# The depthwise conv of a state-space layer as diagonal products on TensorE, with the step's slots laid out anew

## The chip, the cores and the metric

The kernel runs on one core of one Trainium2 chip. A core has five engines that run at the same time and meet through semaphores: TensorE (PE in the profile, with its weight loads listed apart as PEld), VectorE (DVE), ScalarE (ACT), GpSimd (POOL) and SyncE (SP), whose queue issues nearly all transfers here. The metric is the device time of one execution in microseconds, as a median of runs. The kernel before takes 9295.23 us (three runs, 9294.63 to 9299.92).

## The reference, cut to what matters

The network has four layers, each `x = x + layer(groupnorm(x))`, on an input of 8 samples, 384 channels and 32x32 positions: a state-space layer (layer 0), a deformable conv (layer 1), a state-space layer with an MLP behind it (layer 2), and a shift layer (layer 3). The change concerns layer 0 alone. Cut to its core, with L = 1024 tokens, 768 inner channels and 16 states, it is:

```python
xin, z = split(xseq @ in_proj_w.T)                 # 768 channels each
xc = causal_depthwise_conv(xin, conv_w, taps=3) + conv_b
u = silu(xc)
dt, Bm, Cm = split(u @ x_proj_w.T)                 # 24, 16, 16
dt = softplus(dt @ dt_proj_w.T + dt_proj_b)
h[t] = exp(dt[t] * A) * h[t-1] + dt[t] * u[t] * Bm[t]   # per channel and state
y[t] = sum_n h[t, n] * Cm[t, n] + u[t] * D
out = (y * silu(z)) @ out_proj_w.T
```

## The kernel before, in words

**Steps, groups, units.** `ssm_layer` serves both state-space layers. It goes through 16 steps, one for each half (512 tokens) of each of the 8 samples; the first half of a sample is a step with `h` 0, the second one with `h` 1, which carries states and a two-token halo over from the first. A step has six groups `j`, each of 128 inner channels, and a group has eight units `m`. A unit is 32 channels times four states on the 128 partitions, for two state pairs in a 1024-long row. So a step has 48 units, and layer 0 has 768.

**One unit.** ScalarE makes the decays (`decays`, L494: two exponentials of 128x512 into a PSUM tile `da`, of which there are two, taken in turn). GpSimd makes the inputs (`inputs`, L502, a 128x1024 product into `db`, three buffers) and in a step with `h` 1 adds the carry (`add_carry`, L487). VectorE does the recurrence over both (`scan`, L514). Then the states are multiplied by C (`with_c`): by GpSimd (L525) when `m` is in the group's set in `GP_C`, else by VectorE (L527). For GpSimd's units the scan writes to an SBUF tile `hs` (seven buffers); for VectorE's it writes in place in `da`, and the product goes to `hs`. TensorE sums the states of four units into `y` (`read_out`, L537; eight products of 32 columns). The decays of unit i+2 and the inputs of unit i+3 are issued in unit i.

**What is done beside the units.** `plan` gives every other piece of work a slot, 0 to 47, one slot a unit, and an engine queue. All four compute engines take their instructions in exactly that order (`manual_schedule`); in a slot ScalarE's items stand ahead of the decays, VectorE's items behind the scan and the product, TensorE's items ahead of a read-out. Read-outs stand at the end of the slot of unit 5 and of unit 0 of the next group. The items of one step `s` belong to the steps before (`prev`) and after (`nxt`) as well:

- softplus of group j+2 (L408 to L451): `dt_proj` on TensorE in unit 2, four activations in unit 3, `soft_rest` on VectorE in 4, the logarithm in 5; in layer 0 TensorE sums its three parts with an identity matrix (`soft_add`), ScalarE copies the sum out (`soft_take`) and VectorE multiplies it by u (`soft_du`). `spread` then sends both to DRAM and reads them back in the units' layout.
- the gate of group j (`z_proj`, three products; `gate`, silu with a table load, L550; `exp_ln` loads the table of the exponential again, L377), and `close` (L557), which multiplies `y` by it, in unit 2 of the next group.
- for the next step: load and group norm of x, `inner` (L348, three products of 128x128 by 128x512 for each of six channel blocks d), the conv, `silu`, `x_proj`, `x_store` and `load_bc`.
- for the step before: `residual` (load of x), `out_proj` (six products for each of three blocks o) and `out_take` (L589).

**The conv** before is `conv_last` on ScalarE (L352: tap 2 and the bias from PSUM; in a step with `h` 1 three one-column corrections with the halo, L360; in one with `h` 0 the halo is saved, L354) and `conv` on VectorE (L368: two `scalar_tensor_tensor` over 511 and 510 columns, with taps 1 and 0). The same two functions do the first step, ahead of the units, and all of layer 2.

**PSUM.** `da` has two tiles of two banks, `y` one bank, and the pool behind `psum()` three banks, shared by all other products; a new one waits until an old one has been read.

Of the kernel before, what the change touches and what calls it, by code (L numbers as in the profile page):

```python
# [8 lines left out]
F32 = mybir.dt.float32  # L9
AF = mybir.ActivationFunctionType  # L10
ALU = mybir.AluOpType
# [4 lines left out]
P = 128  # L16
# [6 lines left out]
ND = DI // P  # L23
# [3 lines left out]
TS = L // 2  # L27
# [4 lines left out]
IP = P // NI  # L32
NSUB = P // IP
NQP = NS // NI // 2
GP_C = {0: ((0, 2, 4, 6), (0, 2, 5)), 2: ((0, 2, 5), (0, 2, 5))}
PE_SUM = (0,)
ENGINES = {mybir.EngineType.Activation, mybir.EngineType.PE, mybir.EngineType.DVE, mybir.EngineType.Pool}
FF = 4 * C
# [40 lines left out]
V_CW, V_CB, V_DB, V_D, V_A = 0, 18, 24, 30, 36  # L79
# [17 lines left out]
class Net:  # L97
# [107 lines left out]
    def ssm_layer(self, li, src, dst, shift=None):  # L205
        tc, nc, ins = self.tc, self.nc, self.ins
# [4 lines left out]
        with ExitStack() as ctx:  # L211
# [18 lines left out]
            if mlp:  # L230
                w1_d = ins["w1"].rearrange("(k p) o -> p k o", p=P)
                w2_d = ins["w2"].rearrange("(k p) o -> p k o", p=P)
                mean_w = wp.tile([P, P], F32, name="mean_w")
                nc.vector.memset(mean_w, 1.0 / C)
            else:
                win = wp.tile([P, G, 2 * DI], F32, name="win")
                nc.sync.dma_start(out=win, in_=win_d)
                wout = wp.tile([P, ND, C], F32, name="wout")
                nc.sync.dma_start(out=wout, in_=wout_d)
                diag_d = wp.tile([P, ND, P], F32, name="diag_d")  # L240
                for j in range(ND):
                    nc.gpsimd.tensor_scalar(
                        diag_d[:, j, :], self.ident, vec[:, V_D + j : V_D + j + 1], None, ALU.mult
                    )
            nc.sync.dma_start(out=wx, in_=ins[f"wx{li}"].rearrange("(k p) o -> p k o", p=P))
            nc.sync.dma_start(out=wdt, in_=ins[f"wdt{li}"])

# [8 lines left out]
            def v(i):  # L256
                return vec[:, i : i + 1]
# [82 lines left out]
            def inner(s, d):  # L340
                if d == 0:
                    s["u"] = p2.tile([P, ND, TS], F32, name="u", tag="u")
                    if s["h"] == 0:
                        s["sib"]["halo"] = p2.tile([P, ND, 2], F32, name="halo")
                xn, w = s["xn"], s["win", d]
                s["in", d] = ps = self.psum("ps_in")
                for k in range(G):
                    nc.tensor.matmul(ps, w[:, k, :], xn[:, k, :], start=(k == 0), stop=(k == G - 1))  # L348

            def conv_last(s, d):  # L350
                ps, ud = s["in", d], s["u"][:, d, :]
# [152 lines left out]
            def hs_tile(s, m):  # L504
                t = s["hs", m] = p2.tile([P, 2, TS], F32, name="hs", tag="hs", bufs=7)
                return t

            def scan(s, j, m):
                if j == 0 and m == 0 and s["h"] == 0:
                    s["sib"]["st"] = p2.tile([P, ND, NS], F32, name="st")  # L510
                da, db = s["da", m], s["db", m]
                h = hs_tile(s, m) if m in gp_c[j % 2] else da
                h1, da1, db1 = (t.rearrange("p i l -> p (i l)") for t in (h, da, db))
                nc.vector.tensor_tensor_scan(h1, da1, db1, 0.0, ALU.mult, ALU.add)  # L514
                s["h", m] = h
# [5 lines left out]

            def with_c(s, j, m):
                c = s["bc"][m // NSUB][:, 1]
                if m in gp_c[j % 2]:
                    nc.gpsimd.tensor_tensor(s["hs", m], s["hs", m], c, ALU.mult)  # L525
                else:
                    nc.vector.tensor_tensor(hs_tile(s, m), s["da", m], c, ALU.mult)  # L527
# [118 lines left out]

            TG, TS2 = ((8, 8, 24, 24, 31, 47), (24, 31)) if mlp else ((7, 15, 23, 31, 39, 47), (23, 31))
            TZ = (6, 7, 22, 23, 30, 45) if mlp else tuple(t - 1 for t in TG)  # L650
            TI = (16, 17, 18, 24, 25, 26) if mlp else (15, 16, 17, 24, 25, 26)
            NU = NS // 2
            T = ND * NU

            def plan(prev, s, nxt):
                act, dve, pool, pe = queues = [[[] for _ in range(T + NU)] for _ in range(4)]

                def put(q, t, fn, *args):
                    if not args or args[0]:
                        q[t].append((fn, *args))  # L660

                for j in range(ND):
                    t = NU * j
                    put(dve, t + 2, close, *((s, j - 1) if j else (prev, ND - 1)))
                    tz = TZ[j]
                    put(pe, tz - 2, fetch_in, s, ND + j)
                    put(pe, tz, z_proj, s, j)
                    put(act, TG[j], gate, s, j)

                    n, k = (s, j + 2) if j + 2 < ND else (nxt, j + 2 - ND)  # L670
                    put(pe, t + 2, dt_proj, n, k)
                    put(act, t + 3, soft_exp, n, k)
                    put(dve, t + 4, soft_rest, n, k)
                    put(act, t + 5, soft_ln, n, k)
                    if pe_sum:
                        put(pe, t + 5, soft_add, n, k)
                        put(act, t + 6, soft_take, n, k)
                        put(dve, t + 7, soft_du, n, k)
                    else:
                        put(pool, t + 6, soft_sum, n, k)  # L680
                    put(pool, t + 7, spread, n, k)
# [25 lines left out]
                for d, t in enumerate(TI):  # L707
                    put(pe, t - 2, fetch_in, nxt, d)
                    put(pe, t, inner, nxt, d)
                    put(act, t + 1, conv_last, nxt, d)  # L710
                    put(dve, t + 2, conv, nxt, d)
                put(pe, 32 if mlp else 30, x_proj, nxt, 0, ND // 2)
                put(pe, 33 if mlp else 32, x_proj, nxt, ND // 2, ND)
                put(act, 34 if mlp else 33, x_store, nxt)
                for p, t in enumerate((36, 45)):
                    put(pool, t, load_bc, nxt, p)
                put(act, 7 if mlp else 9, residual, prev)
                for o, (t, e) in enumerate(((0, 2), (1, 3), (4, 5)) if mlp else ((8, 9), (10, 11), (12, 13))):
                    if mlp and o < 2:
                        put(pe, (T - 9, T - 6)[o], fetch, nxt and s, "out", o)  # L720
                    else:
                        put(pe, 0, fetch, prev, "out", o)
                    put(pe, t, out_proj, prev, o, 0, ND // 2)
                    put(pe, e, out_proj, prev, o, ND // 2, ND)
                    put(act if mlp else dve, e + (1 if mlp else 2), out_take, prev, o)
# [21 lines left out]
            with tc.manual_schedule(engines=ENGINES):  # L747
# [37 lines left out]
                for i, (s, j, m) in enumerate(units):  # L785
                    c, t = divmod(i, T)
                    if t == 0:
                        queues = plan(
                            steps[c - 1] if c else None, s, steps[c + 1] if c + 1 < len(steps) else None
                        )  # L790
                        for k, q in enumerate(over or ()):
                            for i0, items in enumerate(q):
                                queues[k][i0][:0] = items
                        act, dve, pool, pe = queues
                        over = [q[T:] for q in queues]
                    mine = m in gp_c[j % 2]
                    run(act[t])
                    scan(s, j, m)
                    if not mine:
                        with_c(s, j, m)  # L800
                    keep_last(s, j, m)
                    ahead = units[i + 2] if i + 2 < len(units) else (None, None, None)
                    if ahead[2] == 0:
                        first_token(*ahead[:2])
                    if ahead[0]:
                        decays(*ahead)
                    run(dve[t])
                    if i + 3 < len(units):
                        inputs(*units[i + 3])
                        if ahead[2] == 0:  # L810
                            carry(*ahead[:2])
                            add_carry(*ahead)
                        if units[i + 3][2] > 0:
                            add_carry(*units[i + 3])
                    if mine:
                        with_c(s, j, m)
                    run(pool[t])
                    run(pe[t])
                    for r in late.pop(i, ()):
                        read_out(*r)  # L820
                    if m % NSUB == NSUB - 1:
                        late.setdefault(i + (1 if m == NU - 1 else 2), []).append((s, j, m // NSUB))
# [1113 lines left out]
```

## Time and profile before

The profiled execution took 9297.33 us, of which its instructions span 9295.5 us; 1.8 us lie around them. Layer 0's first scan starts at 75.5 us and its last ends at 2879.5 us.

| stretch (us from the span's start) | length | DVE busy | POOL busy | PE busy | ACT busy | PE clock |
|---|---|---|---|---|---|---|
| whole span | 9295.5 | 83% | 61% | 81% | 70% | 0.88 |
| one step with h 1 (953.29 to 1132.76) | 179.5 | 164.7 | 167.4 | 131.2 | 123.3 | 0.81 |
| one step with h 0 (1132.76 to 1304.90) | 172.1 | 160.2 | 162.2 | 126.6 | 128.3 | 0.81 |

A busy share is a union of instruction spans. TensorE's matmuls are pipelined, and each fp32 product of 128x512 stands in the trace as two records. Start-to-start distances, read off the timeline, are shorter than the durations of the group list, since an instruction's end overlaps the next one's start.

### The profile page before, as it was taken

The numbers are of one execution on the slowest core, as the hardware profiler recorded it, in microseconds if no ns is written. First come the engines' busy times: TensorE is split into PE (matmuls) and PEld (weight loads), VectorE is DVE, ScalarE is ACT, GpSimd is POOL, SyncE is SP. The second block draws the span as 40 slices with busy tenths as digits, with TensorE's granted clock in tenths as the row PEclk, the third lists the DMA queues.
The fourth block names the chain that finished last, engine by engine and source line by source line (L and its number), as shares of the span: only waits on it lengthen the run. The fifth ranks groups of instructions, "written<-read, shape, count | busy, mean of one in ns | idle before, by whom it ended". The sixth has DMA issues, their size and how long they took to land. (4 is left out here: it accounts for less than half of the span.)

```text
span 9295.5 us, 93074 instructions
## 1 busy us (share of the span) xinstructions
PE 7557.6 (81%) x29452; PEld 3856.6 (41%) x29452; DVE 7733.3 (83%) x8617; ACT 6500.3 (70%) x10467; POOL 5645.4 (61%) x3393
## 2 busy tenths in 40 slices
PE   6777677677676999999999997588888888888876
PEld 2222222222223777767777766133333333333333
DVE  6999999999995878878878877788988889898972
ACT  5677677677673878878877876677777677776750
POOL 6999999999994000000000000898989989899964
PEclk7788788788787999999999998798999889999988
DMA  4544544544543333333333333566656666666656
GB/s 123 124 115 113 123 116 114 123 119 114 123 114 81 82 80 85 92 83 85 90 84 86 91 80 85 118 154 151 150 139 155 151 161 147 148 148 145 161 145 112
DMA packets 785233, 1094.47 MB, mean 118 GB/s; under 512 B 274963, under 2 KB 427955, under 8 KB 752985
## 3 DMA queue, kind: packets, MB, share of 16 engines
q1 hardware_dynamic: 722628, 1077.98, 47.6%
q10 hardware_dynamic: 62100, 10.44, 0.7%
q8 instruction: 235, 3.85, 0.2%
q14 instruction: 270, 2.20, 0.1%
HBM read 917.84 MB, written 170.33 MB: 117 GB/s over the span
## 5 line engine op out<-in xcount | busy, mean ns | idle before, releaser
L502 POOL TENSOR_TENSOR db<-dub,bc 128x1024 f32<-128x1024 f32 x1536 | 3603.2, 2355 | 405.9 <-DVE hs L514 224.6
L494 ACT ACTIVATE da<-dtb,vec 128x512 f32<-128x512 f32 x3072 | 2119.5, 691 | 672.9 <-DVE hs L527 416.9
L514 DVE TENSOR_TENSOR_SCAN da<-da,db 128x1024 f32<-128x1024 f32 x912 | 2086.3, 2288 | 258.9 <-ACT da L494 116.4
L435 POOL TENSOR_TENSOR dt<-dt,sp_e 128x512 f32<-128x512 f32 x96 | 122.3, 1274 | 2885.4 <-DMA bc<-bcd 2881.1
L1598 PE MATMUL wacc<-fsm,fxk 128*128 128x221 f32 (+34 forms) x10624 | 1657.2, 315 | 98.1 <-DVE fsm L1568 95.1
L1598 PEld LDWEIGHTS wacc<-fsm,fxk 128*128 128x128 f32 x10624 | 1570.0, 195 | 236.1 <-DVE fsm L1568 159.2
L514 DVE TENSOR_TENSOR_SCAN hs<-da,db 128x1024 f32<-128x1024 f32 x624 | 1423.9, 2282 | 166.4 <-POOL db L487 76.7
L525 POOL TENSOR_TENSOR hs<-hs,bc 128x1024 f32<-128x1024 f32 x624 | 1470.8, 2357 | 15.2 <-ACT st L520 14.9
L1568 DVE TENSOR_TENSOR fsm<-fhy,fhx 128x170 f32<-128x170 f32 (+42 forms) x3216 | 1170.2, 428 | 342.3 <-PE wacc L1598 315.3
L527 DVE TENSOR_TENSOR hs<-da,bc 128x1024 f32<-128x1024 f32 x912 | 1116.9, 1225 | 111.8 <-PE y L537 58.5
L537 PE MATMUL y<-hs,cols 128*32 128x512 f32 x6144 | 826.1, 618 | 160.5 <-POOL hs L525 154.6
L1528 ACT ACTIVATE fhy<-fpyx,cell 128x416 f32<-128x416 f32 (+9 forms) x1280 | 645.5, 576 | 385.0 <-DVE fsm L1568 385.0
L1551 DVE TENSOR_TENSOR fxk<-fxt,fwk 128x1024 f32<-128x1024 f32 (+1 forms) x688 | 787.1, 1179 | 10.2 <-ACT fxt L1330 10.2
L614 PE MATMUL ps_m<-hid,wm 128*128 128x512 f32 x1152 | 550.2, 633 | 61.7 <-ACT hid L609 27.7
L595 PE MATMUL ps_h<-t,wm 128*128 128x512 f32 x1152 | 529.7, 604 | 43.2 <-DVE sp_e L427 25.4
L1533 ACT ACTIVATE fhy<-fhy,cols 128x1344 f32<-128x1344 f32 (+10 forms) x368 | 530.8, 1442 | 12.0
L537 PEld LDWEIGHTS y<-hs,cols 128*32 128x32 f32 x6144 | 171.3, 112 | 798.3 <-issue 497.7
L348 PE MATMUL ps_in<-xn,winr 128*128 128x512 f32 x576 | 328.9, 718 | 174.5 <-ACT xn L337 125.4
L444 PE MATMUL ps_sp<-dt,ident 128*128 128x512 f32 x192 | 168.4, 974 | 290.8 <-ACT dt L414 285.7
L614 PEld LDWEIGHTS ps_m<-hid,wm 128*128 128x128 f32 x1152 | 226.9, 203 | 394.3 <-issue 282.7
L1239 PE MATMUL ps_off<-fxn,fow 128*98 128x465 f32 (+10 forms) x896 | 386.6, 579 | 0.0
L444 PE MATMUL ps_sp<-sp_e,ident 128*128 128x512 f32 x192 | 174.9, 1009 | 259.5 <-DVE sp_e L425 259.5
(212 smaller groups left out, 10436.4 us busy)
## 6 DMA issues: line engine op xcount, KB each, us to landing
dtb<-dtd SPq DMA_DIRECT2D x768, 256.0 KB
dub<-dtd SPq DMA_DIRECT2D x768, 256.0 KB
fpyx<-fposd SPq DMA_DIRECT2D x640, 256.0 KB
wm<-in_w SPq DMA_DIRECT2D x96, 768.0 KB
bc<-bcd SPq DMA_DIRECT2D x256, 256.0 KB
x<-x SPq DMA_DIRECT2D x71, 768.0 KB
dtd<-dt SPq DMA_DIRECT2D x192, 256.0 KB
dtd<-sp_e SPq DMA_DIRECT2D x192, 256.0 KB
```

Of the source, the lines that this page charges most:

```text
L494: nc.scalar.activation(da[:, i, :], s["dtb", j][:, k, :], AF.Exp, scale=na[:, j, n + i : n + i + 1])
L502: nc.gpsimd.tensor_tensor(db, du, s["bc"][p][:, 0], ALU.mult)
L514: nc.vector.tensor_tensor_scan(h1, da1, db1, 0.0, ALU.mult, ALU.add)
L525: nc.gpsimd.tensor_tensor(s["hs", m], s["hs", m], c, ALU.mult)
L527: nc.vector.tensor_tensor(hs_tile(s, m), s["da", m], c, ALU.mult)
L537: nc.tensor.matmul(s["y"][k * IP : (k + 1) * IP, :], sel, s["hs", p * NSUB + k][:, i, :], start=mlp and p == 0 and i == 0, stop=p == NQP - ...
L614: nc.tensor.matmul(ps, s["w2", q][:, f, o * P : (o + 1) * P], s["hid", q][:, f, :], start=(f == 0), stop=(f == 3))
L1528: nc.scalar.activation(hy[:, at : at + (yb - ya) * W], pyx[:, 0, ya * W : yb * W], AF.Abs, bias=bias)
L1533: nc.scalar.activation(hy[:, :at], hy[:, :at], AF.Relu, bias=self.col(Q_ONE), scale=-1.0)
L1551: nc.vector.tensor_tensor(t[:, :n], x, wk[:, j : j + 1, :].to_broadcast([P, n, P]), ALU.mult)
L1568: nc.vector.tensor_tensor(self.sub(sm, at, [(r * w, n), (w, r), (1, w)]), self.sub(hy, hy_at[by] + xa, [(r * W, n), (W, r), (1, w)]), self ...
L1598: nc.tensor.matmul(a[:, ya - 4 * o : yb - 4 * o, xa:xb], k, self.sub(sm, sm_at[by], [(w, yb - ya), (1, w)]), start=False, stop=False,)
```

## The change

In layer 0, for all steps that are planned (not for the first one):

1. **Conv.** ScalarE copies the projection's PSUM tile to u (`conv_in`) and, where `h` is 0, the halo. TensorE multiplies u by three diagonal matrices of the taps, with shifted columns, into a new PSUM tile (`conv_pe`: three products of 128x128 by 512, 511 and 510 columns, and in a step with `h` 1 two more of one and two columns for the halo). ScalarE writes the sum with the bias back to u (`conv_out`). VectorE's `conv` and the one-column corrections go. GpSimd builds the 18 diagonals once at the start.
2. **GP_C.** Groups 0, 2 and 4 gave GpSimd four of their eight products with C, groups 1, 3 and 5 three. Now all six give it three, units 0, 2 and 5; VectorE has the other five. Layer 2 had these sets already and keeps them.
3. **Slots.** Sums of softplus move from unit 5 to 6 of a group and their copy from 6 to 7; gates move from unit 7 to unit 0 of the next group, and their projections from 6 to 7 (the last group's stay in units 5 and 7); the output projection moves from slots 8 to 13 to slots 3 to 9, and `residual` from 9 to 4; the inner projections and the conv are spread over slots 11 to 28, at most one `conv_pe` in a slot; x_proj and x_store come one or two slots later.

```diff
-GP_C = {0: ((0, 2, 4, 6), (0, 2, 5)), 2: ((0, 2, 5), (0, 2, 5))}
+GP_C = {0: ((0, 2, 5),) * 6, 2: ((0, 2, 5),) * 6}
...
+                diag_w = wp.tile([P, 3 * ND, P], F32, name="diag_w")
+                for k in range(3 * ND):
+                    nc.gpsimd.tensor_scalar(
+                        diag_w[:, k, :], self.ident, vec[:, V_CW + k : V_CW + k + 1], None, ALU.mult
+                    )
...
+            def conv_in(s, d):
+                ps, ud = s["in", d], s["u"][:, d, :]
+                nc.scalar.copy(ud, ps)
+                if s["h"] == 0:
+                    nc.scalar.copy(s["sib"]["halo"][:, d, :], ps[:, TS - 2 : TS])
+
+            def conv_pe(s, d):
+                ud = s["u"][:, d, :]
+                s["cv", d] = ps = self.psum("ps_cv")
+                edge = s["h"] == 1
+                nc.tensor.matmul(ps, diag_w[:, 3 * d + 2, :], ud, start=True, stop=False)
+                nc.tensor.matmul(ps[:, 1:], diag_w[:, 3 * d + 1, :], ud[:, : TS - 1], start=False, stop=False)
+                if edge:
+                    halo = s["halo"][:, d, :]
+                    nc.tensor.matmul(ps[:, 0:1], diag_w[:, 3 * d + 1, :], halo[:, 1:2], start=False, stop=False)
+                    nc.tensor.matmul(ps[:, 0:2], diag_w[:, 3 * d, :], halo, start=False, stop=False)
+                nc.tensor.matmul(ps[:, 2:], diag_w[:, 3 * d, :], ud[:, : TS - 2], start=False, stop=True)
+
+            def conv_out(s, d):
+                nc.scalar.activation(s["u"][:, d, :], s["cv", d], AF.Identity, bias=v(V_CB + d))
...
-                h = hs_tile(s, m) if m in gp_c[j % 2] else da
+                h = hs_tile(s, m) if m in gp_c[j] else da
...
-            TG, TS2 = ((8, 8, 24, 24, 31, 47), (24, 31)) if mlp else ((7, 15, 23, 31, 39, 47), (23, 31))
-            TZ = (6, 7, 22, 23, 30, 45) if mlp else tuple(t - 1 for t in TG)
-            TI = (16, 17, 18, 24, 25, 26) if mlp else (15, 16, 17, 24, 25, 26)
+            TG, TS2 = ((8, 8, 24, 24, 31, 47), (24, 31)) if mlp else ((8, 16, 24, 32, 40, 47), (24, 32))
+            TZ = (6, 7, 22, 23, 30, 45) if mlp else (7, 15, 23, 31, 39, 45)
+            TI = (16, 17, 18, 24, 25, 26) if mlp else (11, 12, 17, 18, 20, 24)
+            TCV, TCO = (13, 16, 19, 21, 25, 27), (15, 17, 20, 22, 26, 28)
...
-                        put(pe, t + 5, soft_add, n, k)
-                        put(act, t + 6, soft_take, n, k)
+                        put(pe, t + 6, soft_add, n, k)
+                        put(act, t + 7, soft_take, n, k)
                         put(dve, t + 7, soft_du, n, k)
...
-                    put(act, t + 1, conv_last, nxt, d)
-                    put(dve, t + 2, conv, nxt, d)
-                put(pe, 32 if mlp else 30, x_proj, nxt, 0, ND // 2)
-                put(pe, 33 if mlp else 32, x_proj, nxt, ND // 2, ND)
-                put(act, 34 if mlp else 33, x_store, nxt)
+                    if mlp:
+                        put(act, t + 1, conv_last, nxt, d)
+                        put(dve, t + 2, conv, nxt, d)
+                    else:
+                        put(act, t + 1, conv_in, nxt, d)
+                        put(pe, TCV[d], conv_pe, nxt, d)
+                        put(act, TCO[d], conv_out, nxt, d)
+                put(pe, 32, x_proj, nxt, 0, ND // 2)
+                put(pe, 33, x_proj, nxt, ND // 2, ND)
+                put(act, 34, x_store, nxt)
...
-                put(act, 7 if mlp else 9, residual, prev)
-                for o, (t, e) in enumerate(((0, 2), (1, 3), (4, 5)) if mlp else ((8, 9), (10, 11), (12, 13))):
+                put(act, 7 if mlp else 4, residual, prev)
+                for o, (t, e) in enumerate(((0, 2), (1, 3), (4, 5)) if mlp else ((3, 4), (5, 5), (8, 9))):
```

More of the change, by code (lines that the diff above doesn't have):

```diff
@@ L523, in with_c @@
                 c = s["bc"][m // NSUB][:, 1]
-                if m in gp_c[j % 2]:
+                if m in gp_c[j]:
                     nc.gpsimd.tensor_tensor(s["hs", m], s["hs", m], c, ALU.mult)
@@ L795, in ssm_layer @@
                         over = [q[T:] for q in queues]
-                    mine = m in gp_c[j % 2]
+                    mine = m in gp_c[j]
                     run(act[t])
```

## The prediction

> **What bounds layer 0 now.** First the page: busy time, and the slices of 232 us.
>
> ```profile
> PE 7557.6 (81%) x29452; PEld 3856.6 (41%) x29452; DVE 7733.3 (83%) x8617; ACT 6500.3 (70%) x10467; POOL 5645.4 (61%) x3393
> ...
> DVE  6999999999995878878878877788988889898972
> ...
> POOL 6999999999994000000000000898989989899964
> ```
>
> In slices 2 to 12, layer 0, VectorE and GpSimd are both at nines, while TensorE is at 6 or 7. The chain that ended last is 1% long and lies in layer 3, so it says nothing here. Next the stretches: two whole steps (the first with `h` 1, the second with `h` 0), then groups 1 and 3 of the second one. Columns: length, busy us of PE, PEld, DVE, ACT and POOL, granted clock, DMA share, GB/s.
>
> ```profile
> 953.29:1132.76 179.47, 131.17 (x415) 47.39 (x418) 164.66 (x120) 123.30 (x203) 167.35 (x122) 0.81 0.49 118
> 1132.76:1304.90 172.14, 126.58 (x374) 41.46 (x370) 160.17 (x109) 128.31 (x236) 162.15 (x73) 0.81 0.49 118
> ...
> 1157.83:1186.84 29.01, 27.88 (x85) 10.34 (x84) 27.40 (x19) 20.81 (x37) 29.01 (x13) 1.00 0.47 118
> 1217.21:1249.78 32.57, 25.19 (x67) 8.11 (x66) 29.81 (x24) 25.11 (x48) 27.38 (x13) 0.79 0.44 105
> ```
>
> VectorE is idle for some 12 to 15 us of a step. The groups of instructions of twelve steps (430 to 2539.4 us) give durations:
>
> ```profile
> L502 POOL TENSOR_TENSOR db<-dub,bc 128x1024 f32<-128x1024 f32 x577 | 1353.0, 2357 | 111.5 <-DVE hs L514 83.1 <-DVE da L514 16.6 <-DMA dub<-dtd 11.7
> ...
> L525 POOL TENSOR_TENSOR hs<-hs,bc 128x1024 f32<-128x1024 f32 x252 | 594.1, 2358 | 1.1 <-ACT st L520 0.9
> ...
> L368 DVE SCALAR_TENSOR_TENSOR u<-ps_in,vec,u 128x511 f32<-128x511 f32 x72 | 53.3, 741 | 0.0
> ```
>
> Where VectorE's idle time comes from shows the timeline, at the border of groups 2 and 3 of the step with `h` 0:
>
> ```profile
> 1217.21 2.28 DVE L514 TENSOR_TENSOR_SCAN hs<-da,db 128x1024 f32<-128x1024 f32 x1
> 1221.83 2.30 DVE L514 TENSOR_TENSOR_SCAN da<-da,db 128x1024 f32<-128x1024 f32 x1 [2.34 <-POOL db L502]
> ...
> 1215.03 1.28 ACT L550 ACT_TABLE_LOAD   x1
> 1216.85 0.60 ACT L550 ACTIVATE sz<-ps_z 128x512 f32<-128x512 f32 x1 [0.54 <-PE ps_z L546]
> 1217.35 1.48 ACT L374 ACTIVATE u<-u 128x1536 f32<-128x1536 f32 x1
> 1218.84 1.28 ACT L377 ACT_TABLE_LOAD   x1
> ...
> 1220.33 1.42 ACT L494 ACTIVATE da<-dtb,vec 128x512 f32<-128x512 f32 x2
> ```
>
> The scan's 2.34 us are put down to GpSimd, but the decays it reads end at 1221.75 and it starts at 1221.83: it waited for ScalarE, which had the gate, the silu and two table loads ahead of them. The gate itself waited for `z_proj` (63 us over 72 gates). So VectorE and GpSimd bound layer 0 together, now the one, now the other, and the gate adds a stall at most group borders.
>
> **What the skill says.** The Trainium skill, "TensorE: Matmul & The Clock Gate", Part 1: the clock is half or full, and full after some 3.4 us of sustained work. The timeline agrees, two equal products apart:
>
> ```profile
> 1044.65 2.74 PE L348 MATMUL ps_in<-xn,win 128*128 128x512 f32 x6
> ...
> 1057.63 4.48 PE L348 MATMUL ps_in<-xn,win 128*128 128x512 f32 x6 [4.56 <-ACT dt L414]
> ```
>
> Records start 0.43 us apart in the warm run and 0.85 in the cold part of the other, so an fp32 product costs 0.86 or 1.71 us. "ScalarE: Activation LUTs", What ACT_TABLE_LOAD costs: about 1283 ns; the trace has 1.28. "SBUF — State Buffer", Who interferes with whom: a VectorE instruction with at most one SBUF input does not contend with GpSimd. `conv` and the scan read PSUM and one SBUF tile, so GpSimd gains nothing but its own three products; its 2.36 us in both rows agree. "PSUM — Partial Sum Buffer", Specifications: eight banks; 4 + 1 + 3 are taken, so the conv's new tile shares the three.
>
> **The cost, part by part.** Starts read off the timeline: scan to product 2.33 us, scan to anything else 2.20, product 1.14, `close` 0.58, `soft_rest` 0.59, `soft_du` 0.60, out_take 0.58, three norm statistics 1.79, a conv pair 1.44; GpSimd 2.31 a product, and 0.27 more with a carry.
>
> VectorE, a group after: 5 x 2.33 + 3 x 2.20 + 5 x 1.14 + 1.77 = 25.7 us. Six groups and three out_takes make 156; a step with `h` 1 adds 4.3 for statistics: 160. By the same prices it is 160.8 and 165.1 now (the stretches show 160.2 and 164.7): six conv pairs leave (-8.6) and three products come (+3.6). GpSimd: 66 products instead of 69, 152.5 (`h` 0) and, with 48 carries and six small ones, 167 (`h` 1), down from 159.4 and 174.
>
> ScalarE: `conv_last` (0.79 to the next start) and, in half of the steps, three corrections of 0.29 become a copy of about 0.6 (as L447) and an Identity of about 0.65: within 0.5 us of even, and it has 44 us of slack a step.
>
> The gates. In unit 0, counted from the last product's end: decays 1.42, table 1.28, silu 0.60, table 1.28, saved state 0.19, decays 1.42 = 6.2 us; VectorE needs them after 0.60 + 2.20 + 2.33 + 1.14 = 6.3. So a plain gate fits, one with the silu of u (1.48) stalls 1.4, twice a step, and the last, in unit 7 with `soft_take` beside it, some 0.8. The wait for `z_proj` goes: the read-out now stands ahead of the sums, and the gate comes a slot later. Stalls: about 3.6 us, where the step with `h` 0 has 9 of this kind now (1.3 to 2.3 at five borders).
>
> TensorE. Warm, the conv adds 18 x 0.86 = 15.5 us a step, the halo 12 products of two records at 0.11 (the norm's one-column products) = 2.6. The tightest group is 2: eight blocks of 2.58 (three conv, three projections, sums, gate), 0.86, halo 1.3, two read-outs of 1.72 and the D product 0.86, ten switches at 0.1: 28 us against a group of 26 to 27. Group 1 needs 25, group 0 21 (27 with the norm). TensorE then runs one to two microseconds late by the end of group 2. Late next is `soft_du`, behind the sums in VectorE's queue by one slot now, and the gate. I take 2.4 us a step; 0 if it stays within the slack, and if cold see below. The waits for buffers lie one engine's slot behind their release in the built order, and cost nothing more warm.
>
> Hidden: 18 more diagonals at 0.58 us (six took 3.50) end near 19 us, while GpSimd has nothing to do until 73 us. On SP's queue `residual` in a step with `h` 1 still waits for the norm statistics of slot 2 (11.6 us once a pair of steps) with the readback of dt behind it, as before, so group 0 there stays near 31 us. Its load had two slots to land and has two.
>
> Sum. `h` 0: 156.1 + 3.6 + 2.4 = 162.1, from 172.1. `h` 1: group 0 VectorE 31.2, five groups at GpSimd's 27.9, 1.2 left: 171.9, from 179.5. The first 15 steps (eight, seven) save 80 + 53; the last, with no conv, about 3. 9297.3 (the profiled time, 2.1 over the median of the runs shown) less 136 gives 9161; I say 9160.
>
> **Rivals.** (a) The stalls only move: VectorE keeps its 12 us of idle time in `h` 0, and 5 remain in `h` 1. 168 and 175.5, saving 33 + 28 + 3: 9234. For it: the same in-order queues, one slot for `soft_du`. (b) No stalls: 156 and 170.5, saving 129 + 63 + 3: 9102. (c) TensorE becomes the bound, and it ends slower. At the mean clock of today, 0.81, groups 1 and 2 need 31 and 35 us, four and eight over, and in `h` 1 they need 31 and 33 against 28; a pair of steps then takes 334 + 20 = 354, over today's 351.6: 9297 + 18 = 9315. It decides from a mean clock under about 0.83 in groups 1 and 2. Against it: group 1 in the stretch above, with PE at 27.9 of 29.0, was granted 1.00; dense work is warm. For it: sums wait in order (276 us of weight-load waits over twelve steps have soft_rest as their releaser), and a wait lets the clock fall. Entirely cold conv would cost 31 us a step instead of 15.5. (d) That the change is not done: the built program has 372 more TensorE rows, so it is.
>
> **Numbers.** Forecast (9120 to 9200) 0.45; (a) 0.20; (b) 0.12; no change 0.04; (c) 0.19. Under 0.2% (19 us) no measurement of this kernel tells a change from none. Faster is 0.77, same 0.04, slower 0.19. The range of 9095 to 9290 holds the forecast, (a), (b) and no more.
>
> **What would show it.** VectorE near 156 and 160 us busy a step; walls near 162 and 172; GpSimd at nines in `h` 1 and idle some 10 us in `h` 0; groups 1 and 2 at clock 1.00; scans that wait no more than 1.5 us at the borders of groups 2/3 and 3/4. I am wrong if scans or `soft_du` wait on ps_sp or on hs read-outs by several microseconds in group 2, or if its clock is under 0.83.

## The result, and the profile after

The kernel after takes 9199.95 us (median of four runs, 9189.61 to 9204.01), beside 9295.22 us for the kernel before (four runs, 9294.63 to 9299.92). The ratio is 0.9895, with a 95% interval of 0.9878 to 0.9912: faster by 95 us. The forecast was 9160 us, with 9120 to 9200 for its own mechanism and 9095 to 9290 over all. The median lies in both, but in the narrower one only just: two of the four runs are over 9200.

The profiled execution took 9201.11 us with a span of 9199.3 us. Layer 0's scans now run from 75.2 to 2771.2 us, where they ran from 75.5 to 2879.5: 2696.0 us instead of 2804.0. The gain there is 108.0 us. All that follows, which is unchanged code, takes 6428.1 us instead of 6416.0 and gives 12.1 back.

The busy time of the page of the kernel after, and its slices of 230 us:

```profile
PE 7770.7 (84%) x30184; PEld 3951.7 (43%) x30184; DVE 7663.4 (83%) x8485; ACT 6486.9 (71%) x10413; POOL 5548.4 (60%) x3363
...
DVE  6999999999994877877877875898988889888872
...
POOL 7999999999991000000000000998989989899964
PEclk8999899999988999999999997799999889898988
```

TensorE works 213 us more, VectorE 70 us and GpSimd 97 us less. Both of the latter are still at nines throughout layer 0: the pair that bounded it still does in most groups, with less to do. TensorE's clock is at eight or nine there.

The same two kinds of step as before, in the stretches of the kernel after: the step with `h` 1, the step with `h` 0 behind it, then of the first its groups 0 and 2, and of the second its group 2. Columns as in the prediction: length, busy us of PE, PEld, DVE, ACT and POOL, granted clock, DMA share, GB/s.

```profile
919.50:1093.50 174.00, 143.29 (x440) 53.26 (x441) 159.64 (x113) 124.64 (x208) 159.85 (x117) 0.88 0.50 121
1093.50:1257.70 164.20, 144.03 (x443) 49.20 (x436) 155.34 (x101) 125.82 (x226) 156.25 (x71) 0.92 0.52 124
919.50:956.80 37.30, 29.48 (x89) 14.41 (x88) 30.91 (x31) 17.71 (x32) 28.07 (x22) 0.72 0.37 95
984.20:1011.90 27.70, 27.70 (x87) 10.76 (x86) 25.67 (x16) 23.48 (x41) 27.15 (x21) 1.00 0.52 135
1147.20:1175.30 28.10, 28.10 (x97) 11.69 (x97) 25.64 (x17) 22.50 (x41) 26.88 (x12) 1.00 0.51 122
```

A step with `h` 0 went from 172.1 to 164.2 us, one with `h` 1 from 179.5 to 174.0. VectorE is busy 155.3 and 159.6 us in them. The two groups 2 hold three convs each: TensorE is busy there from one end to the other, at full clock. In the second of them VectorE is busy for 25.64 and GpSimd for 26.88 of 28.10 us, so there TensorE sets the pace, as doubling the conv shows further down; the forecast had summed 28 us for it. Group 0 of the step with `h` 1 is 37.3 us long, at a clock of 0.72, and VectorE, the busiest engine in it, is busy for 30.9.

The conv's products in the timeline of the kernel after (start, length, engine, line; each fp32 product is two records):

```profile
1000.98 1.02 PE L365 MATMUL ps_cv<-u,diag_w 128*128 128x512 f32 x2
1001.84 1.02 PE L366 MATMUL ps_cv<-u,diag_w 128*128 128x511 f32 x2
1002.70 1.02 PE L371 MATMUL ps_cv<-u,diag_w 128*128 128x510 f32 x2
```

They follow one another by 0.86 us, the price the forecast gave a full-clock product.

Now the border of groups 2 and 3 of the step with `h` 0, VectorE and then ScalarE in the timeline of the kernel after:

```profile
1174.70 0.69 DVE L477 TENSOR_TENSOR sp_e<-ps_sp,u 128x512 f32<-128x512 f32 x1 [1.67 <-ACT dt L473]
...
1182.38 2.29 DVE L540 TENSOR_TENSOR_SCAN hs<-da,db 128x1024 f32<-128x1024 f32 x1 [1.35 <-ACT da L520]
...
1174.09 0.58 ACT L473 COPY dt<-ps_sp 128x512 f32<-128x512 f32 x1 [2.75 <-PE ps_sp L470]
...
1176.20 1.28 ACT L576 ACT_TABLE_LOAD   x1
1177.49 0.60 ACT L576 ACTIVATE sz<-ps_z 128x512 f32<-128x512 f32 x1
1177.99 1.48 ACT L400 ACTIVATE u<-u 128x1536 f32<-128x1536 f32 x1
```

The gate no longer waits for `z_proj`, and a gate with the silu of u costs VectorE 1.35 us where it cost 2.34. But `soft_du` waits 1.67 us: the sums on TensorE come late, and it starts only as ScalarE's copy of them ends.

Last, what made group 0 of the step with `h` 1 long, in the timeline of the kernel after, TensorE first and then VectorE:

```profile
925.57 1.99 PE L595 MATMUL ps_o<-u,wout 128*128 128x512 f32 x3
935.38 4.00 PE L145 MATMUL gn_ps<-gn_mv,gmat 128*128 128x2 f32 x18 [7.82 <-DVE gn_mv L137]
939.25 10.19 PE L595 MATMUL ps_o<-u,wout 128*128 128x512 f32 x18
949.27 1.02 PE L560 MATMUL y<-u,diag_d 128*128 128x512 f32 x2
950.22 1.92 PE L563 MATMUL y<-hs,cols 128*32 128x512 f32 x16
952.08 1.12 PE L470 MATMUL ps_sp<-dt,ident 128*128 128x512 f32 x2
...
935.13 0.34 DVE L137 BATCH_NORM_AGGREGATE gn_mv<-gn_st 128x2 f32<-128x12 f32 x3
...
952.16 1.23 DVE L553 TENSOR_TENSOR hs<-da,bc 128x1024 f32<-128x1024 f32 x1 [3.95 <-PE y L563]
955.57 0.69 DVE L477 TENSOR_TENSOR sp_e<-ps_sp,u 128x512 f32<-128x512 f32 x1 [2.19 <-ACT dt L473]
```

TensorE stands 7.82 us in front of the norm's mean, until VectorE has aggregated the norm's statistics (from 935.13 on). Nine products of the output projection, which the change moved here from slots 8 to 13, are queued behind it, and the read-out behind them. VectorE then waits 3.95 us for the read-out to free an `hs` buffer, and 2.19 us for the copy of the sums: 6.1 us, and the group is 6.0 us longer than the 31.2 forecast. The norm's 18 small records take 4.00 us and are 0.21 us apart, twice the 0.11 that the forecast took for such records at full clock; the first six records of the projection behind them start 0.85 to 0.99 us apart, the rest mostly 0.43.

The wait itself is not new. In the timeline of the kernel before, in group 0 of the step with `h` 1 that starts at 953.29 us, TensorE and then VectorE:

```profile
970.56 4.00 PE L145 MATMUL gn_ps<-gn_mv,gmat 128*128 128x2 f32 x18 [14.32 <-DVE gn_mv L137]
...
980.33 1.93 PE L537 MATMUL y<-hs,cols 128*32 128x512 f32 x16
...
982.27 1.23 DVE L527 TENSOR_TENSOR hs<-da,bc 128x1024 f32<-128x1024 f32 x1 [0.77 <-PE y L537]
```

TensorE stood 14.32 us there and did the norm's records in the same 4.00 us, but only the sums and the product with D stood between the norm and the read-out, which started 27.0 us into the step, and VectorE waited 0.77 us for it. Now it starts 30.7 us into the step. New are the nine products between the norm and the read-out.

### The profile page after: what moved, and what is told of

It reads as the page before. It is cut to its first block, busy times and chain, and to the rows that moved or that the text cites. A ratio compares the mean times of both kernels' runs of the same rounds, so it can differ in the third digit from the quotient of the medians.

```text
span 9199.3 us, 94093 instructions
## 1 busy us (share of the span) xinstructions
PE 7770.7 (84%) x30184; PEld 3951.7 (43%) x30184; DVE 7663.4 (83%) x8485; ACT 6486.9 (71%) x10413; POOL 5548.4 (60%) x3363
## 3 DMA queue, kind: packets, MB, share of 16 engines
q8 instruction: 241, 3.95, 0.2%
## 5 line engine op out<-in xcount | busy, mean ns | idle before, releaser
L528 POOL TENSOR_TENSOR db<-dub,bc 128x1024 f32<-128x1024 f32 x1536 | 3605.9, 2357 | 380.4 <-DVE hs L540 172.4
L540 DVE TENSOR_TENSOR_SCAN da<-da,db 128x1024 f32<-128x1024 f32 x960 | 2193.5, 2285 | 130.6 <-ACT da L520 90.4
L540 DVE TENSOR_TENSOR_SCAN hs<-da,db 128x1024 f32<-128x1024 f32 x576 | 1315.3, 2284 | 194.4 <-POOL db L513 80.0
L551 POOL TENSOR_TENSOR hs<-hs,bc 128x1024 f32<-128x1024 f32 x576 | 1357.0, 2356 | 34.3 <-ACT st L546 34.1
L553 DVE TENSOR_TENSOR hs<-da,bc 128x1024 f32<-128x1024 f32 x960 | 1175.6, 1225 | 134.0 <-PE y L563 84.5
L563 PE MATMUL y<-hs,cols 128*32 128x512 f32 x6144 | 966.8, 644 | 291.0 <-POOL hs L551 266.8
L563 PEld LDWEIGHTS y<-hs,cols 128*32 128x32 f32 x6144 | 190.0, 113 | 1009.2 <-issue 497.1
L640 PE MATMUL ps_m<-hid,wm 128*128 128x512 f32 x1152 | 550.6, 633 | 61.7 <-ACT hid L635 27.7
L353 PE MATMUL ps_in<-xn,winr 128*128 128x512 f32 x576 | 326.5, 713 | 174.1 <-ACT xn L342 125.6
L1547 ACT ACTIVATE fhx<-fpyx,cell 128x544 f32<-128x544 f32 (+8 forms) x640 | 380.0, 666 | 0.0
L621 PEld LDWEIGHTS ps_h<-t,wm 128*128 128x128 f32 x1152 | 216.9, 193 | 363.9 <-issue 272.4
```

Source lines behind the costliest of these rows:

```text
L528: nc.gpsimd.tensor_tensor(db, du, s["bc"][p][:, 0], ALU.mult)
L563: nc.tensor.matmul(s["y"][k * IP : (k + 1) * IP, :], sel, s["hs", p * NSUB + k][:, i, :], start=mlp and p == 0 and i == 0, stop=p == NQP - ...
L621: nc.tensor.matmul(ps, s["w1", q][:, k, f * P : (f + 1) * P], s["t"][:, k, :], start=(k == 0), stop=(k == G - 1))
L640: nc.tensor.matmul(ps, s["w2", q][:, f, o * P : (o + 1) * P], s["hid", q][:, f, :], start=(f == 0), stop=(f == 3))
```

## The experiments

The table gives all runs. Beside the medians it has, from the profiled execution, the time of layer 0's scans, the mean length of its steps (of `h` 0 without the first one), and the time of all behind layer 0, which no kernel here changes: that part varied between 6413.5 and 6428.2 us with no order that I could find, so layer 0's own time is the cleaner measure for differences of a few microseconds. The kernels ran on several chips, each beside the kernel before, whose median was 9294.1 to 9296.9 us on them; the ratios are to that one.

| kernel | median us | ratio to before (95%) | layer 0 | h 0 | h 1 | rest |
|---|---|---|---|---|---|---|
| before | 9295.2 | 1 | 2804.0 | 172.0 | 179.3 | 6416.0 |
| GP_C alone | 9337.4 | 1.0046 (1.0029 to 1.0062) | 2845.6 | 177.8 | 180.5 | 6413.9 |
| conv alone | 9271.9 | 0.9976 (0.9967 to 0.9985) | 2777.6 | 174.4 | 174.0 | 6414.3 |
| slots alone | 9270.1 | 0.9976 (0.9966 to 0.9986) | 2778.5 | 168.2 | 180.0 | 6413.5 |
| slots and GP_C | 9282.0 | 0.9985 (0.9978 to 0.9992) | 2786.8 | 170.6 | 179.7 | 6415.8 |
| conv and slots | 9227.3 | 0.9924 (0.9907 to 0.9941) | 2726.9 | 163.1 | 178.2 | 6422.0 |
| after: all three | 9200.0 | 0.9895 (0.9878 to 0.9912) | 2696.0 | 164.2 | 174.1 | 6428.1 |
| norm behind projection | 9163.9 | 0.9855 (0.9839 to 0.9872) | 2671.7 | 164.2 | 170.5 | 6418.0 |
| ten idle products | 9170.2 | 0.9866 (0.9849 to 0.9882) | 2675.5 | 164.2 | 171.1 | 6414.1 |
| copy ahead of gate | 9186.2 | 0.9880 (0.9864 to 0.9897) | 2692.8 | 163.0 | 174.9 | 6418.1 |
| norm and copy | 9173.7 | 0.9866 (0.9849 to 0.9882) | 2674.5 | 163.1 | 172.1 | 6421.4 |
| norm, copy, variance later | 9171.3 | 0.9862 (0.9846 to 0.9879) | 2671.8 | 163.1 | 171.8 | 6428.2 |
| conv twice | 9364.1 | 1.0073 (1.0056 to 1.0090) | 2869.5 | 178.3 | 182.7 | 6416.6 |

### GP_C alone

```diff
-GP_C = {0: ((0, 2, 4, 6), (0, 2, 5)), 2: ((0, 2, 5), (0, 2, 5))}
+GP_C = {0: ((0, 2, 5), (0, 2, 5)), 2: ((0, 2, 5), (0, 2, 5))}
```

> The kernel before with GP_C changed alone (three of eight products with C on GpSimd in every group), conv and slots as before. My theory (both engines bound, the dearer one of a group sets the pace): VectorE has 3.4 us more a step (164 and 169), GpSimd 7 less, idle time of some 12 us stays, so nothing is gained or it is slower: 9290 to 9350. Rival (GpSimd alone is the bound): 7 us less a step, 9185.

The median lies in the range of my theory, far from the rival's 9185. Layer 0 takes 41.6 us more. VectorE, with three more products and the conv still on it, takes the step with `h` 0 from 172.0 to 177.8 us, and `h` 1, where the rival would have had a gain, takes 1.2 us more.

### The conv alone, in the old slots

```diff
+                        put(act, t + 1, conv_in, nxt, d)
+                        put(pe, t + 2, conv_pe, nxt, d)
+                        put(act, t + 4 - (d == 5), conv_out, nxt, d)
```

> The kernel before with the conv on TensorE alone: GP_C and all other slots as before, the copy one slot after the projection, the diagonal products one later, the sum out two later. My theory: VectorE loses 8.6 us a step, GpSimd stays at 159 and 174, so the step with h 0 gains some 4 to 8 us and the one with h 1 some 2: 9220 to 9260. Rival (TensorE in the old slots becomes late, three conv blocks in a row beside the projections): nothing gained or slower, 9295 to 9350.

9272 is 12 us over the range of my theory and 23 us under that of the rival, so neither held alone. The gain is all in `h` 1 (179.3 to 174.0 us), where I had looked for the smaller part. VectorE is busy only 152.3 us in a step with `h` 0, where it was busy for 160.2, but the step is 174.4 us long. Late in group 3 of one and at the border to group 4, ScalarE and then VectorE in the timeline of this kernel:

```profile
1226.24 0.69 ACT L374 ACTIVATE u<-ps_cv,vec 128x512 f32<-128x512 f32 x1 [4.17 <-PE ps_cv L371]
1229.26 0.69 ACT L374 ACTIVATE u<-ps_cv,vec 128x512 f32<-128x512 f32 x1 [2.33 <-PE ps_cv L371]
...
1237.32 0.60 ACT L576 ACTIVATE sz<-ps_z 128x512 f32<-128x512 f32 x1 [1.98 <-PE ps_z L572]
...
1231.45 2.30 DVE L540 TENSOR_TENSOR_SCAN da<-da,db 128x1024 f32<-128x1024 f32 x1 [5.33 <-ACT da L520]
...
1242.30 2.30 DVE L540 TENSOR_TENSOR_SCAN da<-da,db 128x1024 f32<-128x1024 f32 x1 [3.75 <-issue]
```

ScalarE takes its items in order too. It stands 4.17 and 2.33 us before two `conv_out` whose products TensorE has not done, and 1.98 us before a gate for `z_proj`; the decays are queued behind each, and VectorE waits for them. (The second of its two waits is put down to "issue", but the decays that this scan reads end at 1242.22, just ahead of it.) So with the old slots the conv's gain turns into new waits, in `h` 0 all of it.

### The slots alone, and slots with GP_C

Both keep the new slots and put the conv back on VectorE; the first also restores the old `GP_C`, as in the diff of the next experiment.

```diff
-                        put(act, t + 1, conv_in, nxt, d)
-                        put(pe, TCV[d], conv_pe, nxt, d)
-                        put(act, TCO[d], conv_out, nxt, d)
+                    put(act, t + 1, conv_last, nxt, d)
+                    put(dve, t + 2, conv, nxt, d)
```

> The changed kernel with the conv back on VectorE and GP_C as before: the new slots alone. My theory: gates later and sums behind the read-out take some 5 us of scans' waits from each step, and the output projection behind the norm's mean gives some 5 back in steps with h 1: 9250 to 9280. Rival (the slots are worth nothing without the conv on TensorE): 9295.

> The changed kernel with the conv back on VectorE, GP_C and slots as changed. My theory: VectorE has 164 and 169 us of work a step, with some 6 of stalls and the norm's stall 170 and 181: 9270 to 9310, so that the conv is worth 70 us or more. Rival (the conv is worth little, the slots and the balance do it): within 25 us of the changed kernel, 9200 to 9225.

Both fell in their ranges, and the second rival's 9200 to 9225 is out. The slots alone give 25.5 us of layer 0, all in `h` 0 (168.2); group 0 of `h` 1 is already 37.1 us long with them. So that long group comes with the slots and not with the conv. From slots and `GP_C` to all three, the conv is worth 90.8 us of layer 0.

### The conv and the slots, with the old GP_C

```diff
-GP_C = {0: ((0, 2, 5),) * 6, 2: ((0, 2, 5),) * 6}
+GP_C = {0: ((0, 2, 4, 6), (0, 2, 5)) * 3, 2: ((0, 2, 5),) * 6}
```

> The changed kernel with GP_C as before (four products on GpSimd in groups 0, 2 and 4). My theory: VectorE 152 and 157, GpSimd 159 and 174, so GpSimd bounds: about 166 and 180 a step, 9230 to 9270. Rival (the balance does not matter once VectorE is free of the conv): 9200.

9227 is just under the range. The rival's 9200 is not reached: the balance does matter. `h` 1 is 178.2 us, and GpSimd bounds a part of it (group 3 takes 30.0 us with GpSimd at 29.4, where it takes 27.7 with the even `GP_C`). `GP_C` is worth 30.9 us of layer 0 here, costs 8.3 with the slots alone, and 41.6 by itself. In the new slots, then, it pays only with the conv off VectorE; the conv with the even `GP_C` in the old slots was not run. The conv and the slots save 26.4 and 25.5 us alone, and 77.1 together. Beside the conv alone, the slots are the only difference: VectorE is as busy in a step with `h` 0 (152.1 and 152.3 us), and the step takes 163.1 instead of 174.4 us.

### The norm's mean behind the output projection

The mean goes to TensorE one slot later, behind the projection of blocks 0 and 1, and the items that follow from it up to the second mean move by one slot.

```diff
-                    put(pe, 4, lambda n: n.update(gn_ps=self.gn_mean(n["gn_mv"])), nxt)
+                    if mlp:
+                        put(pe, 4, lambda n: n.update(gn_ps=self.gn_mean(n["gn_mv"])), nxt)
...
+                if not mlp and nxt and nxt["h"] == 0:
+                    put(pe, 5, lambda n: n.update(gn_ps=self.gn_mean(n["gn_mv"])), nxt)
```

> The changed kernel with the norm's first TensorE sum one slot later, behind the output projection's first two blocks instead of ahead of most of them, and the norm's next three pieces one slot later. My theory (in steps with h 1 TensorE stands 8.4 us at that sum, its clock falls to half, and read-out and sums come late, which costs VectorE 6 us in group 0): group 0 falls from 37.2 to about 31.5, 40 to 50 us in all, 9150 to 9165. Rival (group 0 of these steps is set by the readback of dt, which waits on SP's queue for the load of x): 9195 to 9205.

The step that starts at 914.0 us, TensorE and then VectorE in the timeline of this kernel:

```profile
917.35 12.46 PE L595 MATMUL ps_o<-u,wout 128*128 128x512 f32 x24
934.04 3.29 PE L145 MATMUL gn_ps<-gn_mv,gmat 128*128 128x2 f32 x18 [4.23 <-DVE sp_e L451]
...
942.25 1.12 PE L470 MATMUL ps_sp<-dt,ident 128*128 128x512 f32 x2
...
945.75 0.69 DVE L477 TENSOR_TENSOR sp_e<-ps_sp,u 128x512 f32<-128x512 f32 x1 [1.72 <-ACT dt L473]
```

TensorE does all 12 products of the first two blocks before the wait; in the kernel after nine of them stood behind it. VectorE's wait for the read-out is gone, the group takes 32.95 us instead of 37.2, and layer 0 gets 24.3 us shorter. The rival, that the readback of dt sets this group, falls. The kernel has the lowest median of the study: 9163.92 us (9161.05 to 9167.62). That this lies in the range I gave is in part luck: I had expected 40 to 50 us from layer 0 and a group of 31.5, and some 10 of the 36 us come from the layers that do not change.

### Ten idle products ahead of the norm's mean

Order and clock both change with the last experiment. This one leaves the order and gives TensorE ten products in slot 3 of the same steps; they go to a PSUM tile that nothing reads, so they add work and change no output.

```diff
+            def busy(s):
+                ps = self.psum("ps_fill")
+                for k in range(FILL):
+                    nc.tensor.matmul(ps, self.ident, diag_d[:, 0:4, :].rearrange("p a b -> p (a b)"), start=(k == 0), stop=(k == FILL - 1))
...
+                        put(pe, 3, busy, nxt)
```

> The changed kernel with ten idle products of 128x128 by 128x512 (own PSUM tile, result not used) on TensorE ahead of the output projection in slot 3 of steps with h 1, so that it is at work while it would wait for the norm statistics. If the fallen clock is what makes the output projection, read-out and sums late (nine products of 0.86 us more when cold), group 0 loses its stall: 9150 to 9170, with more TensorE work. If the order alone does it (all stands behind the norm's sum, at any clock), 9195 to 9215.

30 us faster than after by the medians, 20.5 us in layer 0. The step that starts at 1251.4 us, TensorE in the timeline of this kernel:

```profile
1254.78 10.40 PE L359 MATMUL ps_fill<-diag_d,ident 128*128 128x512 f32 x20
1265.02 2.74 PE L601 MATMUL ps_o<-u,wout 128*128 128x512 f32 x6
1267.59 2.07 PE L146 MATMUL gn_ps<-gn_mv,gmat 128*128 128x2 f32 x18
1269.52 7.97 PE L601 MATMUL ps_o<-u,wout 128*128 128x512 f32 x18
...
1278.28 1.93 PE L569 MATMUL y<-hs,cols 128*32 128x512 f32 x16
```

The norm's mean starts 16.2 us into the step, no earlier than in the kernel after (15.9). But it takes 2.07 us instead of 4.00, and the nine products behind it 7.97 instead of 10.19: 4.1 us, about the 3.95 that VectorE had waited. It works within the seven steps of this kernel too: the mean clock from 12 to 30 us after the start was 1.00 in four, and their group 0 took 33.4 to 33.6 us; 0.91 in two (35.0 us) and 0.81 in one (36.6), where the idle products had run out 3.1 us too soon. Without them the clock was 0.62 to 0.67 and the group 37.0 to 38.1 us. So with the order kept, the length of the group follows the clock, and the clock is worth some 3.6 us of it.

### The copy of the sums ahead of the last gate

In slot 47 ScalarE had the gate first and `soft_take` behind it, in each step.

```diff
-                    put(act, TG[j], gate, s, j)
...
+                for j in range(ND):
+                    put(act, TG[j], gate, s, j)
```

> The changed kernel with the copy of the softplus sums ahead of the gate in slot 47, where both stand in one slot. My theory: soft_du waits 1.6 us there for the copy, which waits for the gate's table load; that goes in steps with h 0, some 1 to 1.6 us each, and less with h 1: 9180 to 9195. Rival (the gate then comes later and the scan waits instead): 9197 to 9205.

The median fell in the range, but layer 0 gains only 3.2 us; the rest of the 14 lies in the unchanged layers. Group 5 of `h` 0 goes from 27.8 to 26.1 us as expected, but group 0 of `h` 1 behind it from 37.3 to 38.7. So the median does not confirm the theory: the rival's mechanism takes back most of the gain.

### Norm and copy together, and the variance one slot later

First the last two edits, of the norm and of the copy, in one kernel.

> The changed kernel with both of the last edits: the norm's sum behind the output projection, and the copy of the sums ahead of the last gate. If the two stalls are separate (group 0 of steps with h 1; the end of group 5), the savings add: some 36 and 14 us, 9145 to 9158. Rival (the earlier copy makes the next step's group 0 late, whose scan then waits for the gate): no more than the norm's part, 9160 to 9170.

At 9173.7 us it gains nothing over the norm's move alone; in layer 0 it is 2.8 us slower. The step with `h` 1 that starts at 911.7 us, VectorE in the timeline of this kernel:

```profile
915.78 2.30 DVE L540 TENSOR_TENSOR_SCAN da<-da,db 128x1024 f32<-128x1024 f32 x1 [1.79 <-ACT da L520]
```

The gate, now behind the copy, holds up the decays of the next group's unit 1 by about what the copy had gained (the 1.6 us that `soft_du` had waited). My theory of additive savings fell, and the rival's mechanism is what the trace shows, though the median is 4 us over the rival's range as well. The last kernel adds the variance of the norm in slots 9 and 10 instead of 8 and 9:

```diff
-                    put(dve, 8, lambda n: n.update(gn_var=self.gn_sum(n["gn_grp"][0], n["gn_ps"])), nxt)
+                    put(dve, 8 if mlp else 9, lambda n: n.update(gn_var=self.gn_sum(n["gn_grp"][0], n["gn_ps"])), nxt)
```

> The last kernel but one (both edits) with the norm's variance on VectorE one slot later, 9 instead of 8, and its root on ScalarE in 10. If VectorE's wait of 1.4 us for the norm's second TensorE sum at the start of group 1 in steps with h 1 counts, 5 to 10 us under the kernel with both edits. If GpSimd bounds those groups, so that it is hidden: within 3 us of it.

It differs by 2.4 us, within the scatter of either (9162.81 to 9176.91 and 9161.55 to 9177.81), and by 0.3 us in a step with `h` 1: the wait for the variance in group 1 was nearly all hidden. What hides it is not shown.

### The conv's products twice

Each block's products run twice and their sum is halved by the copy, so TensorE does the conv's work twice for the same output.

```diff
+                for n in range(2):
+                    first, last = n == 0, n == 1
...
+                nc.scalar.activation(s["u"][:, d, :], s["cv", d], AF.Identity, bias=v(V_CB + d), scale=0.5)
```

> The changed kernel with every diagonal product done twice into the same tile and the sum halved, so that TensorE has 15.5 us more of full-clock work a step (18.1 with the halo in half of them), in groups 1 to 3. My theory (TensorE has some 1 to 2 us of slack in group 2 and some in the others, and dense work stays at full clock): groups 1, 2 and 3 go to 27, 33 and 28, 6 to 12 us a step, 9290 to 9390. Rival (TensorE has room everywhere): within 20 us of the changed kernel. Rival (TensorE is the bound already): all of it shows, 15.5 us a step or more, 9430 and over.

The median lies in the range of my theory and in neither rival's, though the step with `h` 0 grows by more than the 6 to 12 us I gave. Steps grow by 14.1 (`h` 0) and 8.7 us (`h` 1). The groups 2 of a step with `h` 1 and one with `h` 0, in the stretches of this kernel:

```profile
1046.02:1080.52 34.50, 34.50 (x104) 13.80 (x103) 26.07 (x17) 22.57 (x41) 27.84 (x22) 1.00 0.48 122
1218.55:1255.73 37.18, 37.18 (x128) 16.48 (x127) 26.06 (x17) 22.40 (x41) 25.71 (x11) 1.00 0.47 114
```

They hold nine more products, 7.7 us at 0.86, and the second, which prepares a step with `h` 1, the six for the halo, 1.3 us more. They are 6.8 and 9.1 us longer than in the kernel after: in `h` 0 no spare time is left there, in `h` 1 some 0.9 us. Group 1, with 2.6 us of added products (3.0 with the halo in `h` 0), grows by 2.0 to 3.0; group 3, with 5.2, by 2.0 in `h` 0 and not at all in `h` 1.

## Why the prediction was right, and where its sizes were off

**The bound and the direction: right.** VectorE was busy 155.3 us a step in `h` 0 (156 forecast) and 159.6 in `h` 1 (160). In groups 2, 3 and 4 of `h` 1 GpSimd is busy 27.1 to 27.2 of 27.6 to 27.7 us (27.9 forecast). Freeing VectorE paid in `h` 0 only with slots that let it be used: with the same work on it, a step took 174.4 us in the old slots and 163.1 in the new ones.

**The gates: right.** 1.4 us each at borders 2/3 and 3/4 were forecast; 1.35 and 1.61 were measured, and no gate waits for `z_proj` there. Over layer 0, gates waited 84.4 us for it before and 9.7 after.

**Stalls in `h` 0: 8.9 us where 6.0 were summed.** TensorE's lateness was put at 2.4; in group 2 VectorE waits 1.67 for the copy of the sums and 0.55 for decays, 2.2 in all. The term that was too small is the last gate, 0.8: `soft_du` at the end of group 5 waits 1.64 us, since the copy stands behind the gate in slot 47; with the copy first that wait is gone, and comes back in the next group. The rest is 0.36 in group 1 and gaps of 0.2 and less, at which the sum had put nothing. As VectorE is busy 0.7 us less than summed, steps are 2.1 us over the forecast.

**Group 0 of `h` 1: the step that failed.** "So group 0 there stays near 31 us" looked only at `residual` on SP's queue; "group 0 21 (27 with the norm)" priced TensorE's work at full clock. I hadn't named what is queued behind the norm's mean, although the change moves nine products in front of the read-out there. It cost 6.0 us: VectorE waits 3.95 us for the read-out, which the idle products show to be mostly work at half clock, and 2.19 for the copy of the sums. The other five groups took 136.8 us where 139.5 were summed, and the 1.2 left over was not needed, which leaves 2.1 over for the step. That the step came out so near is luck: an error of 6.0 us met two smaller ones the other way.

**The sum.** Eight and seven steps at 2.1 us make 32 us less gain than 133; the last step gained 7.0 instead of 3, as in all kernels with the even `GP_C` (its time is 161.2 to 162.6 us there and 168.3 in the others). So 108 us of layer 0 instead of 136. The other 12 us between 9161 and 9201 lie in layers the change does not touch. Three small readings of the forecast are off without moving it: three more products cost VectorE 3.8 us at its prices (3 x 1.14 and 3 x 0.13), not 3.6; the waits at the five borders were 1.3 to 2.5 us, not 2.3; and two rows of one kernel at 2.36 us do not test whether GpSimd is held up by the conv. The kernel after does: its products on GpSimd take 2357 and 2354 ns with the conv gone.

**The signs.** VectorE's busy times and the clock in groups 1 and 2 (1.00) came as named, the steps are 2.1 us over theirs. The scan at the border of groups 3 and 4 waits 1.61 us where at most 1.5 were named, GpSimd is idle 8.0 us in `h` 0 (some 10 named), and in `h` 1 it is not at nines all the time: it is idle for 9 of the 37.3 us of group 0. The wait of several microseconds for a read-out, named for group 2 as a sign of being wrong, came in group 0.

**The rivals.** Group 2 is where (c) would have decided, and it was close: TensorE is busy in it without a break and in `h` 0 bounds it, and doubling the conv makes the kernel slower than before by 0.73%. But groups 1 to 3 ran at clock 1.00, far from the 0.83 that (c) needed, and so TensorE was not the bound of a step. (a), with 168 and 175.5 us, and (b), with 156 and 170.5, lie on either side of the steps measured. The norm's move brings `h` 1 to (b)'s 170.5 and layer 0's gain to 132.3 us, near the 136 forecast: what was missing from the sum over layer 0 was mostly the work behind that one wait.

**The skill on the clock.** The Trainium skill, "TensorE: Matmul & The Clock Gate", section "HAM oscillation — how this bites in real kernels", describes work that restarts at half clock behind each long wait. This trace agrees. Its Part 1 gives some 3.4 us of sustained work until full clock. In the kernel before, behind the wait of 4.56 us that the prediction shows, it took about that: records lay 0.43 us apart after 3.5 us. Here, behind the wait of 7.82 us, records stayed at the half-clock distance from 935.38 to 943.65, 8.3 us (the granted clock is 0.50 up to there and 1.00 behind it); for this kernel the measured time decides. But the first 3.9 us of it were the norm's records of two columns: from the first record of 512 columns it was 4.4 us, and 4.2 to 6.1 in the seven steps of this kind. Whether the narrow records count as work for the clock is not shown.

## What to carry to other kernels

When work is moved within in-order queues, list for every wait on the path what the move puts behind it, and price that work at the clock it will find there: here nine products behind a wait on TensorE took 10.19 us where they took 7.97 with the clock kept up. Where independent products can stand ahead of such a wait, try that first; here a change of one slot was worth 24 us of layer 0.

A new balance between two engines that bound a kernel together can look like a loss when it is measured alone (41.6 us here) and be a gain once one of them has been freed (30.9 us in place).

## What was not expected of the hardware

Ten products whose result nobody reads made the kernel faster by 20 us in layer 0, with the order of all other work kept: they kept TensorE's clock up over a wait. And layers whose code does not change differed by up to 15 us between the kernels; in layer 2, nearly all steps with `h` 1 behind the first took about 204.6 or about 207.9 us. What decides between these two is left open.
